# One copy for both value banks, early rows for two groups of expert blocks, and the last closing's transfers on another queue

## The chip, the cores and the metric

The kernel runs on one core of one Trainium2 chip. The core has a matrix engine (TensorE, PE in the profile), a vector engine (VectorE, DVE), an activation engine (ScalarE, ACT), a general engine (GpSimd, POOL) and an engine that mostly issues transfers (SyncE, SP). Each works through its own instructions in order, and they wait for one another by semaphores. The metric is the device time of one launch in microseconds (us); lower is better.

## What is computed

Two images of 256 channels and 3136 positions each go through two layers; all data are 32-bit floats. The first layer is a convolutional attention without softmax, which the kernel folds into one 256x256 matrix per image. The second is a transformer block over the 3136 positions as tokens:

```python
t = tokens(x)                                      # (2, 3136, 256)
# causal attention, 4 heads of 64
qkv = layernorm(t) @ W_attn
att = softmax(where(causal, q @ k.T / 8, lowest))
t = t + (att @ v) @ W_proj
# 8 experts, each token through its best two
probs = softmax(layernorm(t) @ gate_w + gate_b)
top2_vals, top2_idx = top_k(probs, 2)
for e in range(8):
    y = gelu(layernorm(t) @ W1[e] + b1[e]) @ W2[e] + b2[e]
    t = t + cw[:, e] * y                           # cw: top2_vals at top2_idx, else 0
```

The kernel doesn't run all tokens through all experts: it sorts the 12,544 pairs of token and expert into blocks of 128 rows by expert, and runs 102 such blocks in its main loop.

## The kernel before: the parts concerned

**Attention.** For each image `b`, each of 7 stretches `i` of W = 448 queries and each pair of heads `hp`, the kernel goes through blocks `j` of 128 keys. A step makes scores (PE), their exponentials `st` (ACT, from a ring of 5 buffers), adds these into `acc` (DVE), and three steps later multiplies them with the values into `yp` (PE). The matrix engine works on two halves of the keys at a time, so `yp` has two banks, one for each half, which have to be added at the end. `yp` exists once: the next stretch or pair of heads can't begin its values before `yp` has been read. There are 2 x 2 x 7 = 28 such endings, called closings here. (`...` marks cuts.)

```python
psc = pool(att, "psc", bufs=2, space=PSUM)     # scores: two buffers
py = pool(att, "py", bufs=1, space=PSUM)       # yp: one
fst = pool(att, "fst", bufs=5)                 # st
...
def values(n):
    ...
        yps[hp, i] = py.tile([P, 2, 512], F32, tag="y", name=f"yp_{sn}")
    ...
    if last:
        yh = qT[:, hp, i * W : (i + 1) * W]
        nc.scalar.copy(yh, yp[:, 0, :W])                            # L703
        nc.vector.tensor_tensor(yh, yh, yp[:, 1, :W], ALU.add)      # L704
        del yps[hp, i]
        later.append((clock[0], sum_rows, hp, i, yh))

def queue_of(hp, i):
    return nc.gpsimd if (b, hp, i) == (B - 1, NH - 1, NB - 1) else nc.sync
```

What follows a closing is a chain of small steps for the softmax's denominators, each put off by some steps through the list `later`: `sum_rows` sums `acc` over the keys (PE, L720), copies the sums out (ACT, L725) and sends them through HBM to bring them into another layout (L728, L731); `invert` takes the reciprocal (DVE, L740) and sends it back, spread over partitions (L741, L746); `scale` multiplies (DVE, L752); `hand_on` lets the output projection (`project_out`, L602) go on. For the very last of the 28 closings `queue_of` sends all these transfers by GpSimd's queue.

**The last closing, between the expert blocks.** When attention's own loop has ended, the chain of the last closing is run by `closing`, a generator from which `pull` takes pieces; between two expert blocks `meanwhile` pulls two or three pieces:

```python
def closing():
    if not general:
        while finished[B - 1][NH - 1] < N:
            clock[0] += 4
            due(clock[0])        # 1: sum_rows, 2: invert, 3: scale, 4: hand_on
            yield True
            yield True
        while not projected[B - 1]:
            yield False
        queue.append(judge())
    end.close()
    scatter_rows.append(...)
    yield True

def meanwhile():
    scatters = placed[1] and not sent[1]
    pull(3 if scatters or worked[0] >= MIXED else 2)
    ...
```

The pieces that follow are the output projection of image 1's last rows, then `dispatch(1)` (the gate's softmax, the two best experts and each pair's place, all on DVE; `placed[1]` is set at its end), then the scatter of image 1's rows into their places by GpSimd (`sent[1]` at its end). The rows of image 1 are first fetched for block 42, six blocks ahead of use.

**The expert blocks.** The loop over `n`, from -1 on:

```python
for n in range(-1, MAIN + LATE):                       # LATE = 3
    while len(fetched) * GB <= min(n + 6, MAIN - 1):   # GB = 3 blocks in a group
        fetched.append(fetch(len(fetched)))
    ...
    if 0 <= n < MAIN:
        act[n] = hidden(n, xin.pop(n), wb.pop(n))      # PE L1403, ACT gelu L1412
    for m in (n + 1, n + 2):
        ... xin[m] = inputs(m, groups[m // GB])        # PE transposes L1380, ACT copy L1384
    for m in (n + 1, n + 2):
        ... wb[m] = weights(m)                         # DVE copy of the expert's W1, L1391, two buffers
    if 0 <= n - LATE < MAIN:
        outputs(n - LATE, act.pop(n - LATE))           # PE L1422, DVE bias L1432
    ...
    between()                                          # meanwhile

def fetch(g):
    ...
    if g == 0:
        return early_rows, None      # rows of blocks 0 to 2, loaded during attention (tokens, L1659)
    ...
        (nc.sync if g > 2 else nc.scalar).dma_start(   # L1329
            out=xb, in_=xds[b][s * P : e * P].rearrange("(n p) w -> p n w", p=P))
```

The buffers `xb` of the groups from 1 on lie in memory that attention gives back at its end, so their transfers start only then.

Of the kernel before, what the change touches and what calls it, by code (L numbers as in the profile page):

```python
# [27 lines left out]
def conv_attn_moe_kernel(  # L28
# [75 lines left out]
    MIXED = MOST0 + E  # L104
    NBLK = (2 * B * N + E * (P - 1)) // P
    GB = 3

    MAIN = NBLK - GB
    SCALE = 1.0 / HS**0.5
# [333 lines left out]
    def layer1(nm, general):  # L443

        with ExitStack() as whole:
# [170 lines left out]
            def attend(  # L616
# [63 lines left out]
                def values(n):  # L680
                    i, hp, j, first, last, order = steps[n]
                    k = chunk(j)
                    c0 = max(0, j * P - i * W)
                    sn = f"{nm}{b}_{hp}_{i}"
                    st = sts.pop(n)
                    if first:
                        yps[hp, i] = py.tile([P, 2, 512], F32, tag="y", name=f"yp_{sn}")
                    yp = yps[hp, i]

                    for h in range(0, k, HS):  # L690
                        end = last or (h and all(chunk(o) <= h for o in order[order.index(j) + 1 :]))
                        for a in range(2):
                            nc.tensor.matmul(  # L693
                                yp[a * HS : (a + 1) * HS, h // HS, c0:W],
                                v[hp][h : h + HS, j, a, :HS],
                                st[h : h + HS, a, c0:],
                                start=first,
                                stop=bool(end),
                            )
                    if last:  # L700

                        yh = qT[:, hp, i * W : (i + 1) * W]
                        nc.scalar.copy(yh, yp[:, 0, :W])  # L703
                        nc.vector.tensor_tensor(yh, yh, yp[:, 1, :W], ALU.add)  # L704
                        del yps[hp, i]
                        later.append((clock[0], sum_rows, hp, i, yh))

                def queue_of(hp, i):

                    return nc.gpsimd if (b, hp, i) == (B - 1, NH - 1, NB - 1) else nc.sync  # L710

                def sum_rows(hp, i, yh):
                    r = (b * NH + hp) * NB + i
                    sn = f"{nm}{b}_{hp}_{i}"
                    acc = accs.pop((hp, i))
                    sp = bank(f"sp_{b}_{hp}_{i}")

                    flat = acc.rearrange("p a w -> p (a w)")
                    for g in range(4):
                        nc.tensor.matmul(  # L720
                            sp[g * 32 : (g + 1) * 32, : W // 2], ones[:, :32],
                            flat[:, g * W // 2 : (g + 1) * W // 2], start=True, stop=True,
                        )
                    line = fs.tile([P, W], F32, tag="rb", bufs=3, name=f"line_{sn}")
                    nc.scalar.copy(line[:, : W // 2], sp[:, : W // 2])  # L725
                    halves = sum_d[r].rearrange("a (h w) -> (a h) w", h=2)
                    for g in range(4):
                        queue_of(hp, i).dma_start(  # L728
                            out=halves[g : g + 1], in_=line[g * 32 : g * 32 + 1, : W // 2]
                        )  # L730
                    queue_of(hp, i).dma_start(  # L731
                        out=sums[:, r], in_=sum_d[r].rearrange("a (p f) -> (a p) f", p=HS)
                    )
                    later.append((clock[0] + 4, invert, hp, i, yh))

                def invert(hp, i, yh):
                    r = (b * NH + hp) * NB + i
                    sn = f"{nm}{b}_{hp}_{i}"
                    back = fs.tile([P, 2 * W // P], F32, tag="back", name=f"back_{sn}")
                    nc.vector.reciprocal(back, sums[:, r])  # L740
                    queue_of(hp, i).dma_start(  # L741
                        out=inv_d[r].rearrange("a (p f) -> (a p) f", p=HS), in_=back
                    )
                    rb = fs.tile([P, W], F32, tag="rb", bufs=3, name=f"rb_{sn}")
                    for a in range(2):
                        queue_of(hp, i).dma_start(  # L746
                            out=rb[a * HS : (a + 1) * HS], in_=inv_d[r, a].partition_broadcast(HS)
                        )
                    later.append((clock[0] + 4, lambda hp, i, yh: scale(hp, i, yh, rb), hp, i, yh))
# [551 lines left out]
            def experts(w1s, w2s, b2s, ex, es, ps6, between, need, written):  # L1301
# [4 lines left out]
                def fetch(g):  # L1306
                    s, e = g * GB, (g + 1) * GB
                    b = 0 if e <= FULL0 else 1
                    need(b)
                    if g == 0:  # L1310
                        return early_rows, None
                    f = known[b][0]
                    xb = ex.tile([P, GB, xds[b].shape[1]], F32, tag="xb", bufs=3, name=f"xb_{nm}_{g}")
                    if b:
                        at = nc.values_load_multi_w_load_instructions(
                            qblk[0:1, s - f : e - f],
                            engines=(SP,),
                            min_val=0,
                            max_val=NBLK - FULL0 - 1,
                            skip_runtime_bounds_check_because="a permutation's places",  # L1320
                        )[1]
                        table = xds[b].rearrange("(n p) w -> n p w", p=P)
                        for a in range(GB):
                            nc.sync.dma_start(
                                out=xb[:, a],
                                in_=table[bass.ds(at[a], 1)].rearrange("o p w -> p (o w)"),
                            )
                    else:
                        (nc.sync if g > 2 else nc.scalar).dma_start(  # L1329
                            out=xb, in_=xds[b][s * P : e * P].rearrange("(n p) w -> p n w", p=P)  # L1330
                        )
                    mixed = max(0, min(e, MIXED) - s) if b else 0
                    other = None
                    if mixed:
                        other = ex.tile([P, GB, C], F32, tag="xo", bufs=1, name=f"xo_{nm}_{g}")
                        nc.sync.dma_start(
                            out=other[:, :mixed],
                            in_=xds[0][s * P : (s + mixed) * P].rearrange("(n p) w -> p n w", p=P),
                        )
                    return xb, other  # L1340
# [33 lines left out]
                def inputs(n, group):  # L1374
                    xb, to = group
                    g = n % GB
                    rows = xb[g] if n < GB else xb[:, g, :C]
                    tp = ps6.tile([P, 512], F32, tag="tp", bufs=2, name=f"tp_{nm}_{n}")
                    for c in range(NH):
                        nc.tensor.transpose(  # L1380
                            tp[:, c * P : (c + 1) * P], rows[:, c * P : (c + 1) * P], ident
                        )
                    xT = es.tile([P, NH, P], F32, tag="xT", name=f"xT_{nm}_{n}")
                    nc.scalar.copy(xT.rearrange("p c t -> p (c t)"), tp[:, : NH * P])  # L1384
                    return xT, to
# [252 lines left out]
            def tokens(b, qT, done):  # L1638
# [5 lines left out]
                if b == 0:  # L1644
# [8 lines left out]

                    while not read[B - 1]:
                        yield False
                    for n in range(0, GB, 2):
                        m = min(2, GB - n)
                        xb = bg.tile([P, 2, C], F32, tag="xn", name=f"xb_{nm}_first{n}")
                        nc.sync.dma_start(  # L1659
                            out=xb[:, :m],  # L1660
                            in_=xds[0][n * P : (n + m) * P].rearrange("(n p) w -> p n w", p=P),
# [108 lines left out]
            def closing():  # L1770

                if not general:
                    while finished[B - 1][NH - 1] < N:
                        clock[0] += 4
                        due(clock[0])
                        yield True
                        yield True
                    while not projected[B - 1]:
                        yield False
                    queue.append(judge())  # L1780
# [5 lines left out]
            with ExitStack() as moe:  # L1786
# [11 lines left out]
                        )  # L1798
                for _ in load_w2(True):
                    pass  # L1800
                while len(early_rows) < GB:
                    pull()

                def need(b):
# [9 lines left out]
                    queue.appendleft(finish(1, oy, 3))  # L1814

                def meanwhile():
                    scatters = placed[1] and not sent[1]
                    pull(3 if scatters or worked[0] >= MIXED else 2)
                    if side and next(side[0], None) is None:
                        side.popleft()  # L1820

# [179 lines left out]
```

## Time and profile before

| | before |
|---|---|
| time, median of 3 runs | 1307.98 us |
| lowest, highest | 1307.3, 1308.54 us |
| span of the profiled execution | 1331.2 us |
| PE busy | 1276.9 us (96%) |
| DVE busy | 787.7 us (59%) |
| ACT busy | 602.2 us (45%) |
| POOL busy | 306.2 us (23%) |
| mean granted PE clock | 0.989 |

The profile is one execution, recorded by the hardware; the recorded execution is some 23 us longer than the timed ones. Times in it are microseconds from its start, unless a row says mean ns. Attention runs from about 97 to 887 us, the expert blocks from 888 to 1311 us. A row names the engine, the line of the kernel, the operation and the tiles (`out<-in`); in brackets stands for how long the engine had been idle before, and what ended that.

### The profile page before, as it was taken

To read this page: it belongs to the slowest core of one execution; us is meant where nothing else is said; L and a number is where in the kernel's file an instruction comes from. 1 tells how busy PE (TensorE), PEld (TensorE's weight loads), DVE (VectorE), ACT (ScalarE), POOL (GpSimd) and SP (SyncE) were. 2 spreads that over 40 slices of the span, in tenths; PEclk is the share of its full clock that TensorE was granted. 3 is DMA by queue.
4 is the path that set the end of the run, shared out by engine and by line. 5 is a ranking of instruction groups with operands and counts; after the bars stand their busy time and mean duration, and the time that the engine had idled before them with its cause. 6 is when DMAs were issued, how large, how long until landed. Compare 5 with 4: busy or idle time off the path is not lost.

```text
span 1331.2 us, 28014 instructions
## 1 busy us (share of the span) xinstructions
PE 1276.9 (96%) x10569; PEld 808.0 (61%) x10569; DVE 787.7 (59%) x1683; ACT 602.2 (45%) x1226; POOL 306.2 (23%) x297
## 2 busy tenths in 40 slices
PE   8999999999999999999999989989999999899995
PEld 7875444444444444444345434449988999899894
DVE  1582555748777654675768777765744443355553
ACT  0145554555565554455553455553423333244341
POOL 1113110000000111110004461010066212655541
PEclk9999999999999999999999999999999999999997
DMA  9993000000000000100001126141244433556553
GB/s 311 383 326 113 16 24 24 24 16 24 9 17 17 17 2 9 40 9 15 9 8 60 60 80 198 33 138 56 67 144 129 130 109 97 179 175 202 180 156 107
DMA packets 110471, 123.54 MB, mean 93 GB/s; under 512 B 19904, under 2 KB 100045, under 8 KB 110329
## 3 DMA queue, kind: packets, MB, share of 16 engines
q1 hardware_dynamic: 96232, 92.49, 22.4%
q0 software_dynamic: 10272, 26.00, 5.8%
q10 hardware_dynamic: 3824, 3.18, 0.8%
q8 instruction: 87, 1.43, 0.5%
q14 instruction: 56, 0.45, 0.1%
HBM read 62.65 MB, written 60.41 MB: 92 GB/s over the span
## 4 chain that ended last, share of the span: by engine, by line
PE 91%; DVE 3%; issue 2%; ACT 1%; DMA 1%; POOL 0%; DVEq 0%; SPq 0%; POOLq 0%; ACTq 0%
PE yp_f L693 20%; PE sc_f L653 19%; PE ht_f L1403 14%; PE yp_f L1422 13%; PE qk_f L539 7%; PE v_f L558 4%; PE pp_f L602 4%; PE cp L324 3%; PE gram L255 3%; PE tp_f L1380 2%; DVE acc_f L675 1%; ACT st_f L661 1%; PE sp_f L720 1%; PE yo_f L1549 1%; PE xp_f L518 1%
## 5 line engine op out<-in xcount | busy, mean ns | idle before, releaser
L661 ACT ACTIVATE st_f<-sc_f 128x896 f32<-128x896 f32 (+5 forms) x400 | 333.5, 838 | 300.1 <-PE sc_f L653 273.7
L675 DVE TENSOR_TENSOR acc_f<-acc_f,st_f 128x896 f32<-128x896 f32 (+5 forms) x372 | 366.5, 985 | 168.3 <-ACT st_f L661 161.3
L693 PE MATMUL yp_f<-st_f,v_f 64*64 64x448 f32 (+6 forms) x3184 | 340.5, 503 | 9.7 <-DVE qT_f L704 6.5
L653 PE MATMUL sc_f<-qT_f,kT_f 64*64 64x448 f32 (+6 forms) x3184 | 341.5, 500 | 4.0 <-ACT st_f L661 4.0
L1412 ACT ACTIVATE g_f<-ht_f,b1b 128x128 f32<-128x128 f32 x408 | 116.8, 371 | 243.0 <-PE ht_f L1403 127.6
L1403 PE MATMUL ht_f<-xT_f,w_f 128*128 128x128 f32 x1632 | 203.4, 277 | 9.3 <-issue 6.6
L653 PEld LDWEIGHTS sc_f<-qT_f,kT_f 64*64 64x64 f32 x3184 | 116.6, 133 | 156.4 <-issue 134.5
L693 PEld LDWEIGHTS yp_f<-st_f,v_f 64*64 64x64 f32 x3184 | 112.3, 133 | 162.6 <-issue 134.7
L1403 PEld LDWEIGHTS ht_f<-xT_f,w_f 128*128 128x128 f32 x1632 | 198.5, 193 | 14.9 <-issue 10.4
L501 POOL TENSOR_SCALAR xn_f<-t 128x256 f32<-128x256 f32 (+1 forms) x50 | 68.2, 1373 | 542.6 <-issue 330.8
L1284 POOL DMA_INDIRECT x_slots<-xr_f,idx x100 | 113.0, 1130 | 218.7 <-DVE xr_f L1276 116.6
L1391 DVE COPY w_f<-w1s_f 128x1024 f32 x102 | 71.1, 698 | 86.8 <-PE ht_f L1403 38.8
L539 PE MATMUL qk_f<-px_f,wat 128*128 128x512 f32 (+1 forms) x224 | 92.6, 558 | 1.2 <-ACT px_f L524 1.2
L1439 POOL DMA_INDIRECT y_tokens<-ys_f,to_f x60 | 60.3, 1005 | 139.7 <-DVE ys_f L1432 109.8
L1432 DVE TENSOR_TENSOR ys_f<-yp_f,kT_f 128x128 f32<-128x128 f32 x102 | 29.6, 291 | 99.7 <-PE yp_f L1422 65.3
L663 DVE TENSOR_TENSOR st_f<-st_f,keep 128x256 f32<-128x256 f32 (+1 forms) x112 | 44.2, 395 | 68.2 <-ACT st_f L661 67.7
L539 PEld LDWEIGHTS qk_f<-px_f,wat 128*128 128x128 f32 x224 | 38.7, 190 | 54.4 <-issue 45.3
L1422 PE MATMUL yp_f<-px_f,g_f 128*128 x204 | 62.7, 390 | 1.0 <-issue 1.0
L1422 PE MATMUL yp_f<-v_f,g_f 128*128 x204 | 61.5, 382 | 0.8 <-issue 0.8
L1422 PE MATMUL yp_f<-kT_f,g_f 128*128 x204 | 62.1, 386 | 0.0
L1422 PE MATMUL yp_f<-w2s_f,g_f 128*128 x204 | 61.2, 382 | 0.3 <-issue 0.3
L1496 POOL DMA_INDIRECT y_f<-y_slots,idx x50 | 54.8, 1096 | 16.3 <-issue 14.7
(259 smaller groups left out, 1170.8 us busy)
## 6 DMA issues: line engine op xcount, KB each, us to landing
x_slots<-fill SPq DMA_DIRECT2D x1, 8127.0 KB
xb_f<-x_slots SPq DMA_DIRECT2D x60, 129.0 KB
x_slots<-fill SPq DMA_DIRECT2D x1, 7296.0 KB
y_slots<-ys_f SPq DMA_DIRECT2D x57, 128.0 KB
kept<-t SPq DMA_DIRECT2D x2, 3200.0 KB
x<-in_x_dram SPq DMA_DIRECT2D x14, 448.0 KB
xr<-in_x_rows_dram SPq DMA_DIRECT2D x12, 512.0 KB
out_dram<-ot_f SPq DMA_DIRECT2D x24, 256.0 KB
```

The lines of the kernel that those rows point to most:

```text
L501: nc.gpsimd.tensor_scalar(xn[:k, a], ts[b][:k, n + a, :C], ts[b][:k, n + a, MEAN : MEAN + 1], ts[b][:k, n + a, RSTD : RSTD + 1], ALU.subtr ...
L539: nc.tensor.matmul(ps[:, :w], wat[:, c, d0 : d0 + P], xT[:, c, :w], start=(c == 0), stop=(c == NH - 1),)
L653: nc.tensor.matmul(ps[h : h + HS, a, c0:W], kT[hp][rows, j * P + h : j * P + h + HS], qT[rows, hp, q0 + c0 : q0 + W], start=True, stop=True,)
L661: nc.scalar.activation(st[:k, :, c0:], ps[:k, :, c0:W], AF.Exp, scale=SCALE)
L675: nc.vector.tensor_tensor(acc[:k, :, c0:], acc[:k, :, c0:], st[:k, :, c0:], ALU.add)
L693: nc.tensor.matmul(yp[a * HS : (a + 1) * HS, h // HS, c0:W], v[hp][h : h + HS, j, a, :HS], st[h : h + HS, a, c0:], start=first, stop=bool( ...
L1284: s = nc.gpsimd.indirect_dma_start(out=xds[b], out_offset=bass.IndirectOffsetOnAxis(ap=idxs[b][:kk, k, n : n + 1], axis=0), in_=xr[:kk], i ...
L1391: nc.vector.tensor_copy(w, w1s[:, :, bass.ds(e, 1), :].rearrange("p c e h -> p c (e h)"))
L1403: nc.tensor.matmul(ht[:, k, :], w[:, c, k * P : (k + 1) * P], xT[:, c, :], start=(c == 0), stop=(c == NH - 1),)
L1412: nc.scalar.activation(g[:, k, :], ht[:, k, :], AF.Gelu, bias=b1bs[b][:, k, i : i + 1])
L1422: nc.tensor.matmul(yp[:, :C], g[:, k, :], w2s[k][:, bass.ds(e, 1), :].rearrange("p e d -> p (e d)"), start=(k == 0), stop=(k == KH - 1),)
L1439: s = nc.gpsimd.indirect_dma_start(out=y_tokens, out_offset=bass.IndirectOffsetOnAxis(ap=to[:, n % GB : n % GB + 1], axis=0), in_=ys, in_o ...
```

## The change

Three things are changed.

1. **Both banks in one copy.** ACT copies both banks of `yp` at once (128x896) into a buffer `both` from the ring of the `st` tiles, and GpSimd adds the two halves from there into `yh`. DVE has no part in a closing's first step any more. Before, `yp` was free when DVE's addition had ended; now it is free when ACT's copy has.
2. **Early rows for two groups.** The rows of the first six expert blocks, and not three, are loaded during attention. The three more blocks take buffers of the `xn` and `xr` tiles that are idle by then. Group 1 is no longer fetched when attention ends.
3. **The last closing.** Its transfers go by SP's queue like those of all others. `closing` gives six pieces (three blocks) between the sums and the reciprocal, four (two blocks) between the reciprocal and the scaling, and none after that, where it gave two each. To make up for the later start, the sorting of image 1's tokens (`dispatch(1)`) takes three pieces per block from its start on and not only from its scatter on.

```diff
--- before.py
+++ after.py
@@ -104,6 +104,7 @@
     MIXED = MOST0 + E
     NBLK = (2 * B * N + E * (P - 1)) // P
     GB = 3
+    EARLY = 2
 
     MAIN = NBLK - GB
     SCALE = 1.0 / HS**0.5
@@ -700,14 +701,11 @@
                     if last:
 
                         yh = qT[:, hp, i * W : (i + 1) * W]
-                        nc.scalar.copy(yh, yp[:, 0, :W])
-                        nc.vector.tensor_tensor(yh, yh, yp[:, 1, :W], ALU.add)
+                        both = fst.tile([P, 2, W], F32, tag="st", name=f"both_{sn}")
+                        nc.scalar.copy(both, yp[:, :, :W])
+                        nc.gpsimd.tensor_tensor(yh, both[:, 0], both[:, 1], ALU.add)
                         del yps[hp, i]
                         later.append((clock[0], sum_rows, hp, i, yh))
-
-                def queue_of(hp, i):
-
-                    return nc.gpsimd if (b, hp, i) == (B - 1, NH - 1, NB - 1) else nc.sync
 
                 def sum_rows(hp, i, yh):
                     r = (b * NH + hp) * NB + i
@@ -725,10 +723,10 @@
                     nc.scalar.copy(line[:, : W // 2], sp[:, : W // 2])
                     halves = sum_d[r].rearrange("a (h w) -> (a h) w", h=2)
                     for g in range(4):
-                        queue_of(hp, i).dma_start(
+                        nc.sync.dma_start(
                             out=halves[g : g + 1], in_=line[g * 32 : g * 32 + 1, : W // 2]
                         )
-                    queue_of(hp, i).dma_start(
+                    nc.sync.dma_start(
                         out=sums[:, r], in_=sum_d[r].rearrange("a (p f) -> (a p) f", p=HS)
                     )
                     later.append((clock[0] + 4, invert, hp, i, yh))
@@ -738,12 +736,12 @@
                     sn = f"{nm}{b}_{hp}_{i}"
                     back = fs.tile([P, 2 * W // P], F32, tag="back", name=f"back_{sn}")
                     nc.vector.reciprocal(back, sums[:, r])
-                    queue_of(hp, i).dma_start(
+                    nc.sync.dma_start(
                         out=inv_d[r].rearrange("a (p f) -> (a p) f", p=HS), in_=back
                     )
                     rb = fs.tile([P, W], F32, tag="rb", bufs=3, name=f"rb_{sn}")
                     for a in range(2):
-                        queue_of(hp, i).dma_start(
+                        nc.sync.dma_start(
                             out=rb[a * HS : (a + 1) * HS], in_=inv_d[r, a].partition_broadcast(HS)
                         )
                     later.append((clock[0] + 4, lambda hp, i, yh: scale(hp, i, yh, rb), hp, i, yh))
@@ -1307,8 +1305,8 @@
                     s, e = g * GB, (g + 1) * GB
                     b = 0 if e <= FULL0 else 1
                     need(b)
-                    if g == 0:
-                        return early_rows, None
+                    if g < EARLY:
+                        return early_rows[s:e], None
                     f = known[b][0]
                     xb = ex.tile([P, GB, xds[b].shape[1]], F32, tag="xb", bufs=3, name=f"xb_{nm}_{g}")
                     if b:
@@ -1374,7 +1372,7 @@
                 def inputs(n, group):
                     xb, to = group
                     g = n % GB
-                    rows = xb[g] if n < GB else xb[:, g, :C]
+                    rows = xb[g] if n < EARLY * GB else xb[:, g, :C]
                     tp = ps6.tile([P, 512], F32, tag="tp", bufs=2, name=f"tp_{nm}_{n}")
                     for c in range(NH):
                         nc.tensor.transpose(
@@ -1653,9 +1651,12 @@
 
                     while not read[B - 1]:
                         yield False
-                    for n in range(0, GB, 2):
-                        m = min(2, GB - n)
-                        xb = bg.tile([P, 2, C], F32, tag="xn", name=f"xb_{nm}_first{n}")
+                    for n, m in ((0, 2), (2, 2), (4, 1), (5, 1)):
+                        name = f"xb_{nm}_first{n}"
+                        if m == 2:
+                            xb = bg.tile([P, 2, C], F32, tag="xn", name=name)
+                        else:
+                            xb = bg.tile([P, C], F32, tag="xr", name=name).unsqueeze(1)
                         nc.sync.dma_start(
                             out=xb[:, :m],
                             in_=xds[0][n * P : (n + m) * P].rearrange("(n p) w -> p n w", p=P),
@@ -1770,11 +1771,13 @@
             def closing():
 
                 if not general:
+
+                    blocks = deque((3, 2))
                     while finished[B - 1][NH - 1] < N:
                         clock[0] += 4
                         due(clock[0])
-                        yield True
-                        yield True
+                        for _ in range(2 * blocks.popleft() if blocks else 0):
+                            yield True
                     while not projected[B - 1]:
                         yield False
                     queue.append(judge())
@@ -1798,7 +1801,7 @@
                         )
                 for _ in load_w2(True):
                     pass
-                while len(early_rows) < GB:
+                while len(early_rows) < EARLY * GB:
                     pull()
 
                 def need(b):
@@ -1814,8 +1817,8 @@
                     queue.appendleft(finish(1, oy, 3))
 
                 def meanwhile():
-                    scatters = placed[1] and not sent[1]
-                    pull(3 if scatters or worked[0] >= MIXED else 2)
+                    sorting = projected[1] and not sent[1]
+                    pull(3 if sorting or worked[0] >= MIXED else 2)
                     if side and next(side[0], None) is None:
                         side.popleft()
```

## The prediction

> **What bounds the kernel now.** I read the page's shares first, then the waits of PE, then the timeline at the closings, then the chain and the stretches around the end of attention.
>
> ```profile
> PE 1276.9 (96%) x10569; PEld 808.0 (61%) x10569; DVE 787.7 (59%) x1683; ACT 602.2 (45%) x1226; POOL 306.2 (23%) x297
> ```
>
> PE is busy for 1276.9 of 1331.2 us, so 54.3 us is all the idle time there is. The change takes no matrix work away; it can only win back part of these 54.3 us. By the waits of PE, the two parts can reach these rows:
>
> ```profile
> PE yp_f L693 <- DVE qT_f L704: 6.5, 6, 1.5
> PE sc_f L653 <- ACT st_f L661: 4.0, 3, 1.5
> PE ht_f L1403 <- DVE w_f L1391: 2.7, 1, 2.7
> PE tp_f L1380 <- DMA xb_f<-x_slots: 1.1, 1, 1.1
> ```
>
> The columns are total us, times and longest. The first row is the closing's wait for DVE's addition: only 6 of 28 closings leave PE idle. The third and fourth happen once each, just after attention. A closing that does wait, the first (timeline, start and length ahead of the engine; the weight loads of PE left out):
>
> ```profile
> 130.16 0.53 ACT L703 COPY qT_f<-yp_f 128x448 f32<-128x448 f32 x1
> ...
> 130.75 0.82 DVE L675 TENSOR_TENSOR acc_f<-acc_f,st_f 128x640 f32<-128x640 f32 x1
> ...
> 131.50 0.61 DVE L704 TENSOR_TENSOR qT_f<-qT_f,yp_f 128x448 f32<-128x448 f32 x1
> 132.03 0.42 DVE L663 TENSOR_TENSOR st_f<-st_f,keep 128x256 f32<-128x256 f32 x1
> 132.16 0.61 PE L693 MATMUL yp_f<-st_f,v_f 64*64 64x448 f32 x4 [1.49 <-DVE qT_f L704]
> ```
>
> ACT's copy ends at 130.69, but DVE, in order, is in the middle of an `acc` addition, so `yp` is free only at 132.11. In most closings the same release comes 1.76 us after the copy's start, and PE covers it with two score products and the sums (at 316.16 the addition ends at 317.91, and PE goes on at 317.98 without a gap).
>
> The end of attention, from the chain of waits in that stretch:
>
> ```profile
> 889.00 2.10 POOL sums L728 x3
> 891.10 3.76 DMA sums<-line_f
> ...
> 895.52 1.97 DMA sums<-sums
> 897.49 0.02 issue
> 897.51 0.07 DVE back_f L740
> ...
> 897.70 0.71 DVE w_f L1391
> 898.40 0.14 issue
> 898.54 2.99 PE ht_f L1403 x16
> ```
>
> The reciprocal was put into DVE's order right after the sums were sent. It waits until 897.51, and the weight copy of block 3 behind it makes PE wait 2.69 us. A block's hidden layer takes 1.78 us later in the chain; here it takes 2.99, because the granted clock has dropped (stretches: length, then busy time of PE, PEld, DVE, ACT, POOL, then PEclk, DMA share, GB/s):
>
> ```profile
> 894.00:899.00 5.00, 2.31 (x21) 2.10 (x20) 0.88 (x2) 1.71 (x6) 1.14 (x2) 1.00 0.02 1
> 899.00:904.00 5.00, 5.00 (x25) 4.66 (x25) 0.43 (x1) 1.41 (x5) 1.07 (x2) 0.66 0.15 47
> ```
>
> **What the Trainium skill says.** "TensorE: Matmul & The Clock Gate", Part 1: after an idle window the array's clock falls to half and comes back after some 3.4 us of work. The trace agrees: 0.66 in the 5 us after the gap. So a gap costs more than its own length. "DMA: Bandwidth & Descriptors", Latency and other measured facts: the first byte takes about 0.6 us from SP's queue and 1 us from GpSimd's. The trace agrees in direction: an issue of the sums lasts 0.25 us on SP and 0.56 on POOL (medians of L728). "GPSIMD Engine Reference", sections 1 and 3.1: GpSimd can't read PSUM, hence the copy first, and an addition of two 2048-wide tiles takes it 4.5 us against DVE's 2.3. No two-input operation runs on POOL in this trace; its one-input normalisation of 128x256 takes 1.37 us, or 5.3 ns per element. "SBUF — State Buffer", Who interferes with whom: GpSimd and a DVE operation with two inputs block each other. Here DVE's 128x896 additions that overlap a normalisation take 1.08 to 1.24 us, against 1.09 otherwise: little to see.
>
> **Part 1, one copy for both banks.** Removed: 28 DVE additions of 0.615 us, 17 us of an engine with slack. Longer: 28 ACT copies. I take the 128x896 exponential's 0.92 us (mean 918 ns) for the 128x896 copy, against 0.53 before: 28 x 0.39 = 11 us more on ACT, beside PE. Added: 28 POOL additions. By the skill's rate the estimate is 4.5 x 448/2048 = 1.0 us, by this trace's normalisation 448 x 5.3 ns = 2.4 us.
>
> On the path: `yp` is free 0.92 us after the copy's start. For the six closings that wait I take the gain in release (old end of addition, less copy start plus 0.92), at most the recorded wait:
> - at 130.16: 132.11 - 131.08 = 1.03, of a wait of 1.49
> - at 197.25: 1.36, wait 1.02, so 1.02
> - at 515.55: 1.04, of 1.49
> - at 585.83: 1.38, wait 1.02, so 1.02
> - at 634.61: 1.61, wait 0.59, so 0.59
> - at 695.62: 1.88, wait 0.85, so 0.85
>
> The sum is 5.55 us. Weight loads wait for L704 in 14 places, so other closings may lose a tenth each that the modelled ends hide: 0.5 more. Against it: in a closing ACT's exponentials come 0.39 later. In the full-size closing at 316.16 they would end at 318.0 and 319.3, needed at 319.5 and 321.0, so nothing is lost; in the small closings (first stretches, 6 of them) I allow 0.1 each, 0.6. Part 1: -5.5 us.
>
> **Part 2, group 1 early.** It removes the 1.15 us wait of PE for `xb` at 893.4. The first group's early loads are issued at 826.7, 60 us ahead of use; the second group's will stand beside them.
>
> **Part 3, the last closing.** Without gaps, from 888.23 a block's hidden layer and transposes take 2.0 us, and outputs 1.73. Hidden layers 0 to 3 would then run to about 896.3, the outputs of block 0 to 898.1. In the trace these end at 903.99, so 5.9 us can be won: 1.15 (part 2) + 2.69 (weights) + some 2.0 of slow clock (1.2 on the hidden layer, 0.7 on what follows). Does the new order avoid the wait? SP can issue the sums at 888.8. With four issues of 0.25 us and about 2 us to land (the 1.97 above), they arrive about 892; the second transfer about 894.4. The reciprocal now stands behind the weight copy of block 4, which can't start before hidden layer 2 has ended (894.1), so it runs at about 895 with little wait. `inverses` lands at about 897.6 and `rb` near 900.5; the scaling stands behind the bias of block 1 at about 902.3. But nothing is left between scaling and projection: the second of the two projected tiles needs the scaled rows, and I charge 0.4 us. Net for parts 2 and 3: -5.5 us.
>
> The faster sorting: the pieces of `dispatch(1)` took DVE about 20 us in all, two per block; three per block are 2.8 us a block on average, plus weights and bias 1.2, that is 4.0 against PE's 3.73. The worst triple is about 3.7 + 1.2 = 4.9. A weight copy has 5.6 us between its buffer coming free and its use, so I expect this backlog to stay hidden. The dispatch begins one block later and takes about 3.5 fewer, so the scatter should end some 2.5 blocks (9 us) earlier than 1043.5. It was in time before; the gain from that is none.
>
> **Sum.** -5.5 - 5.5 = -11.0 us of profiled time. The timed runs are 23 us shorter than the profile, so some of its waits may be its own; I keep 85%, -9.4, giving 1298.5 us.
>
> **Rivals.** (a) *`both` holds up the ring.* `both` is an extra claim on five `st` buffers and comes back only after POOL's addition. For it: POOL works in order, and its scatters run back to back around the closing at 775. Against it: the buffer is needed again four steps, some 6 us, later. If it bites in half of the closings by 0.5 us, 7 us of the gain are lost: 1305. (b) *ACT becomes the release.* The score buffers are two, and PE already waits 4.0 us for exponentials; 0.39 us more, 28 times, unhidden would be 11 us: about 1309. Against it: ACT idles 0.59 us in each steady step. (c) *SP is no faster.* SP's queue is loaded with weights at 885 to 887, and the transfers keep landing late; then the reciprocal still waits and only parts 1 and 2 count: about 1303. (d) *DVE's heap of sorting pieces starves PE*: 2 to 4 us lost, 1301.
>
> **Range and chances.** Rivals cost singly up to 10 us; the upside is the full idle time of both places, 14 us. So 1294 to 1305. All idle time of PE is only 4% and the reachable part under 1%, so a change over 2% either way is very unlikely: faster 0.02, same 0.97, slower 0.01.
>
> **What would show it.** Right: no PE wait for L704, few for the new copy; the copy near 0.92 us; no PE gap over 0.5 us from 887 to 905 and a clock of 1.00 there; the outputs of block 0 over 5 us sooner after the end of attention; the scatter's end some 9 us earlier. Wrong: ACT waits for POOL's addition at the `st` ring, more PE waits for `st_f` L661, DVE still blocked at L740 or L752, or new gaps between 925 and 960. A gain under 3 us, or a loss, would make the reasoning wrong, and not only its size.

## The result

| | before | after |
|---|---|---|
| time, median of 4 runs each, side by side | 1308.26 us | 1303.21 us |
| lowest to highest | 1307.3 to 1309.54 | 1302.95 to 1303.32 |
| ratio, with its 95% interval | | 0.996 (0.9943 to 0.9978) |
| span of the profiled execution | 1331.2 us | 1301.6 us |

The gain is 5.05 us, 0.4%. The time lies inside the predicted range, but the gain is about half of the 9.4 us predicted.

The profile after answers to the rows shown of before. The page's shares:

```profile
PE 1267.3 (97%) x10569; PEld 802.9 (62%) x10569; DVE 792.2 (61%) x1655; ACT 610.6 (47%) x1226; POOL 344.9 (26%) x317
```

The waits of PE (total us, times, longest):

```profile
PE yo_f L1547 <- DVE y_f L1534: 8.2, 5, 4.9
...
PE xp_f L519 <- POOL xn_f L502: 2.2, 2, 1.2
...
PE sc_f L654 <- ACT st_f L662: 0.9, 2, 0.7
PE yp_f L694 <- ACT both_f L705: 0.9, 2, 0.4
...
PE ht_f L1401 <- ACT xT_f L1382: 0.6, 1, 0.6
```

The waits for DVE's addition, for the weights at the end of attention and for `xb` are gone; what took over is 0.9 us for the new copy and 0.6 for a copy of transposed rows. But the second row shown is new: PE waits for POOL's normalised tiles, and no recording of the kernel before has such a row. No rival had this one.

The first closing (timeline: start, length, in brackets the idle time ahead):

```profile
129.03 0.90 ACT L705 COPY both_f<-yp_f 128x896 f32<-128x896 f32 x1
...
129.98 1.52 PE L694 MATMUL yp_f<-st_f,v_f 64*64 64x448 f32 x16 [0.44 <-ACT both_f L705]
130.01 1.43 POOL L706 TENSOR_TENSOR qT_f<-both_f 128x448 f32<-128x448 f32 x1 [4.93 <-ACT both_f L705]
```

PE goes on 0.95 us after the copy's start, and 2.00 before (132.16 - 130.16). POOL's addition begins as PE's next values do and holds nobody here. Over all 28 it takes 1.30 us on average (36.3 us in all), between the two estimates.

The end of attention (stretches: length, then busy time of PE, PEld, DVE, ACT, POOL, then PEclk, DMA share, GB/s):

```profile
885.00:890.00 5.00, 4.94 (x40) 4.87 (x41) 1.50 (x3) 3.57 (x15) 0.00 (x0) 1.00 0.05 5
890.00:895.00 5.00, 5.00 (x33) 4.63 (x33) 1.45 (x4) 1.96 (x8) 0.00 (x0) 1.00 0.52 138
895.00:900.00 5.00, 5.00 (x34) 4.46 (x33) 3.41 (x10) 1.41 (x5) 0.00 (x0) 1.00 0.12 39
```

No gap is left, at full clock. So both places look as predicted, and yet only half of the time came. The experiments ask where the rest is.

### The profile page after: what moved, and what is told of

Read it like the earlier page. It is cut to its first block, busy times and chain, and to the rows that moved or that the text cites. A ratio compares the mean times of both kernels' runs of the same rounds, so it can differ in the third digit from the quotient of the medians.

```text
span 1301.6 us, 28033 instructions
## 1 busy us (share of the span) xinstructions
PE 1267.3 (97%) x10569; PEld 802.9 (62%) x10569; DVE 792.2 (61%) x1655; ACT 610.6 (47%) x1226; POOL 344.9 (26%) x317
## 4 chain that ended last, share of the span: by engine, by line
PE 89%; DVE 3%; issue 3%; ACT 2%; POOL 2%; DMA 1%; DVEq 0%; POOLq 0%; ACTq 0%; SPq 0%
PE yp_f L694 20%; PE sc_f L654 19%; PE ht_f L1401 13%; PE yp_f L1420 12%; PE qk_f L540 7%; PE v_f L559 4%; PE pp_f L603 4%; PE cp L325 3%; PE gram L256 3%; PE tp_f L1378 2%; PE sp_f L718 1%; ACT st_f L662 1%; PE yo_f L1547 1%; PE xp_f L519 1%; DMA y_f<-y_slots,idx 1%
## 5 line engine op out<-in xcount | busy, mean ns | idle before, releaser
L676 DVE TENSOR_TENSOR acc_f<-acc_f,st_f 128x896 f32<-128x896 f32 (+5 forms) x372 | 375.3, 1009 | 160.0 <-ACT st_f L662 151.0
L1401 PE MATMUL ht_f<-xT_f,w_f 128*128 128x128 f32 x1632 | 199.5, 275 | 0.6 <-ACT xT_f L1382 0.6
L706 POOL TENSOR_TENSOR qT_f<-both_f 128x448 f32<-128x448 f32 x28 | 36.3, 1298 | 522.7 <-ACT both_f L705 522.7
L502 POOL TENSOR_SCALAR xn_f<-t 128x256 f32<-128x256 f32 (+1 forms) x50 | 72.3, 1455 | 143.6 <-DVE t L171 47.2
```

Source lines behind the costliest of these rows:

```text
L502: nc.gpsimd.tensor_scalar(xn[:k, a], ts[b][:k, n + a, :C], ts[b][:k, n + a, MEAN : MEAN + 1], ts[b][:k, n + a, RSTD : RSTD + 1], ALU.subtr ...
L676: nc.vector.tensor_tensor(acc[:k, :, c0:], acc[:k, :, c0:], st[:k, :, c0:], ALU.add)
L1401: nc.tensor.matmul(ht[:, k, :], w[:, c, k * P : (k + 1) * P], xT[:, c, :], start=(c == 0), stop=(c == NH - 1),)
```

## The experiments

The fifth to eighth kernels of the table ran on another chip, on which the kernel before takes 2.3% longer (1337.87 us), so times are compared within a set only.

| kernel | time, us | before in the same set | ratio, 95% interval |
|---|---|---|---|
| before once more | 1307.63 | 1307.97 | 0.9996 (0.9987 to 1.0004) |
| part 1 alone | 1306.15 | 1307.97 | 0.9986 (0.9979 to 0.9992) |
| part 2 alone | 1307.11 | 1307.97 | 0.9995 (0.9987 to 1.0003) |
| part 3 alone | 1305.73 | 1307.97 | 0.9981 (0.9972 to 0.9989) |
| part 3, SP's queue alone | 1337.77 | 1337.87 | 0.9996 (0.9985 to 1.0008) |
| part 3, spacing and sorting alone | 1336.02 | 1337.87 | 0.9985 (0.9973 to 0.9998) |
| after, addition on DVE | 1331.66 | 1337.87 | 0.9959 (0.9945 to 0.9972) |
| after, normalisation first | 1327.09 | 1337.87 | 0.9925 (0.9898 to 0.9952) |
| after once more | 1302.98 | 1307.08 | 0.997 (0.9957 to 0.9982) |
| after, normalisation first, again | 1299.13 | 1307.08 | 0.9939 (0.9926 to 0.9953) |
| the same with eight transfers more | 1296.66 | 1307.08 | 0.9916 (0.9902 to 0.9929) |
| the same with GpSimd's queue in the last closing | 1296.74 | 1307.08 | 0.9923 (0.991 to 0.9937) |

### The kernel before once more

No edit. The recorded execution of before was 23 us longer than the timed ones. This asks which of its waits are the kernel's own (theory A in the texts on record: the waits were read rightly, and the change brings new ones) and which belong to that execution (theory B).

> The kernel before, unchanged, recorded once more. Theory A (the waits were read rightly, and the change itself brings new ones): the recorded span is again near 1331 us, with about 6.5 us of PE waiting for the closing's addition L704, 2.7 for the weights behind the reciprocal and some 9 us of PE idle marked issue in the expert blocks. Theory B (that recorded execution was a disturbed one, 23 us over the timed runs): the span is near 1307 us, the issue rows are gone, and the waits that the change removes are smaller than the 6.5 + 2.7 + 1.1 us read.

Measured: a span of 1306.1 us. The waits of PE in it:

```profile
PE yp_f L693 <- DVE qT_f L704: 8.5, 7, 1.6
...
PE ht_f L1403 <- DVE w_f L1391: 2.5, 1, 2.5
PE tp_f L1380 <- DMA xb_f<-x_slots: 1.4, 1, 1.4
...
PE pp_f L602 <- DVE qT_f L752: 0.7, 1, 0.7
```

and the stretch of the gap at the end of attention:

```profile
890.00:895.00 5.00, 2.51 (x23) 2.30 (x22) 0.88 (x2) 1.40 (x5) 1.14 (x2) 1.00 0.03 1
```

The waits that the change removes are all there, and larger (8.5 us at seven closings, for 6.5 at six). What is not there: the expert blocks' rows of PE waiting for "issue", that is, for nothing that the profile shows (9.7 us in the recorded execution of before: 6.6 for `ht`, 2.1 for the experts' `yp`, 1.0 for `tp`; the row of 6.6 is below), the 4.0 us of waits for exponentials, and a slow clock after the gap; the clock stays at 1.00 through 890 to 905. So the removable waits were the kernel's own, and much of the 23 us was not.

```profile
PE ht_f L1403 <- issue: 6.6, 10, 1.0
```

The slow clock is another matter. It came back after the same gap when part 1 alone was recorded (below), and with part 2 alone too (0.68 in the same stretch); what decided it is in the last section.

```profile
890.00:895.00 5.00, 5.00 (x25) 4.84 (x26) 0.00 (x0) 1.41 (x5) 1.08 (x2) 0.68 0.15 47
```

### Each part alone

Part 1 alone: the copy of both banks and POOL's addition (the diff's lines at L700), all else as before.

> Part 1 alone: both banks in one ACT copy, addition on GpSimd. Theory A: -5.5 us from the closings, +3 to 4 us lost where GpSimd's normalisation now stands behind the addition (PE waits for xn, 2.2 us in the changed kernel's record), so -1.5 to -2.5 us against before. Theory B: below -1.5 us, or a small loss, because the closings' waits were smaller in the timed runs.

Part 2 alone: `EARLY`, the four early loads and the two uses of `early_rows`.

> Part 2 alone: rows of six blocks loaded during attention. Theory A: -1 us at most (PE's one wait for xb, 1.1 us), less if the wait for the weights just behind it grows by as much (then 0). Theory B: 0 us.

Part 3 alone: SP's queue, the spacing of three and two blocks, and the sorting by three pieces.

> Part 3 alone: last closing's transfers on SP, wider spacing, sorting at three pieces. Theory A: -4.5 us (2.7 of waiting for the weights and 2 of slow clock, less 0.3 between scaling and projection). Theory B: -2 to -3 us, because the timed runs lose less there. The wait of PE for xb, 1.1 us, stays in both.

Measured: 1.8, 0.9 and 2.2 us under before. The sum is 4.9 us, about as much as the whole change brings, so the parts add up as far as these intervals tell.

*Part 2* brings nothing that its interval would show. PE's wait for `xb` (1.4 us) is gone, but the next one grows, since the reciprocal that ends it comes no earlier: the wait for the weights is 3.1 us here for 2.5. By the trace 0.8 us is left.

*Part 1* I followed by the starts of the closings' copies, less those of the kernel before once more (negative is earlier). Between the first closing (+0.3) and the thirteenth (-1.8, at 447 us) and again from the fourteenth (+0.6, at 497) to the last (-3.0) time is won: 2.1 and 3.6, that is 5.7. But between the thirteenth and the fourteenth 2.3 us are lost. There image 1 begins, and there is the new wait for POOL. POOL's timeline in the kernel before:

```profile
286.97 2.88 POOL L501 TENSOR_SCALAR xn_f<-t 128x256 f32<-128x256 f32 x2 [44.94 <-PE xp_f L518]
454.17 5.16 POOL L501 TENSOR_SCALAR xn_f<-t 128x256 f32<-128x256 f32 x4 [164.32 <-issue]
```

With nothing else to do, POOL had normalised the second two of image 1's tiles at 287 (and the first two at 239), over 160 us before their use. In the changed kernel:

```profile
445.87 1.25 POOL L706 TENSOR_TENSOR qT_f<-both_f 128x448 f32<-128x448 f32 x1 [39.14 <-ACT both_f L705]
447.11 10.07 POOL L502 TENSOR_SCALAR xn_f<-t 128x256 f32<-128x256 f32 x7
```

In POOL's order the normalisation stands behind the additions of the closings of image 0, down to the thirteenth. POOL idles for 39 us and then has to do it in a hurry, while PE waits twice. (By the closings part 1 wins 3.4 us, and timed 1.8; the recorded execution, 1304.95 us, is 1.2 us faster than the median of its runs.)

*Part 3* I followed by the starts of the bias of each block's output (DVE). The lead over the kernel before is 4.5 us at block 4, about 4.0 at block 13 and from 30 to 58, and then falls to about 2 in blocks 59 to 65, where the first rows of the output are gathered. This second loss is in the changed kernel too (1.3 us there).

### The pieces of part 3

SP's queue alone:

```diff
-    return nc.gpsimd if (b, hp, i) == (B - 1, NH - 1, NB - 1) else nc.sync
+    return nc.sync
```

> The kernel before, with only the last closing's transfers moved from GpSimd's queue to SP's. Theory order (the wait for weights is lost because the reciprocal stands too early in DVE's order): the sums come about 2 us earlier on SP, but the reciprocal still blocks the weight copy of block 3, so PE's wait for weights shrinks from 2.5 us to somewhere from 0.5 to 1.5 and does not go; 1306.5 to 1307.6 us, 0.5 to 1.5 under the kernel before. Theory queue (SP alone does it): the wait is under 0.3 us and the time is that of the last part alone, about 1305.7. And for the 1.8 us that the last part loses again in blocks 59 to 65: if the change of queues brings it, the first gather of finished rows starts over 5 us after block 56's bias here; if not, 3.1 us after, as before.

The spacing and the sorting alone, the transfers still on GpSimd's queue:

```diff
+    blocks = deque((3, 2))
...
-        yield True
-        yield True
+        for _ in range(2 * blocks.popleft() if blocks else 0):
+            yield True
...
-    scatters = placed[1] and not sent[1]
-    pull(3 if scatters or worked[0] >= MIXED else 2)
+    sorting = projected[1] and not sent[1]
+    pull(3 if sorting or worked[0] >= MIXED else 2)
```

> The kernel before, with the last closing's reciprocal and scaling put three and two blocks behind and the sorting pulled three pieces at a time, but its transfers still on GpSimd's queue. Theory order: the wait for weights (2.5 us) goes as in the last part alone; about 1305.7 us, 2.0 to 2.5 under the kernel before, unless the later landing makes DVE stand before the reciprocal: then up to 1 us less is won. Theory queue: the sums land at 897.5 as before, DVE waits there, and PE waits 1 us or more for a later weight copy: 1306.5 or more. And for the 1.8 us lost again in blocks 59 to 65: if the earlier sorting brings it, the first gather of finished rows starts over 5 us after block 56's bias here; if the queues do, 3.1 us after.

Measured: nothing (0.9996) for the queue, 1.85 us for the spacing. The waits of PE at the end of attention, first with the queue alone, then with the spacing alone:

```profile
PE ht_f L1403 <- DVE w_f L1391: 1.8, 1, 1.8
```

```profile
PE tp_f L1380 <- DMA xb_f<-x_slots: 1.9, 1, 1.9
```

With SP's transfers 1.8 us of the wait for weights stay (a little more than I had expected); with the spacing that wait is gone, and the only larger one is that which part 2 removes. So it is the place of the reciprocal in DVE's order that counts. The intervals of the two timings overlap, and it is the traces that tell them apart; the spacing and the sorting were not run singly. And the second loss: the first gather starts 5.75 us after block 56's bias with the queue alone, 3.14 with the spacing alone. It comes with the queue, not with the sorting.

### The addition on DVE, and the normalisation first

After, with the two banks added by DVE from `both`:

```diff
-    nc.gpsimd.tensor_tensor(yh, both[:, 0], both[:, 1], ALU.add)
+    nc.vector.tensor_tensor(yh, both[:, 0], both[:, 1], ALU.add)
```

> The changed kernel, with the closing's addition of the two copied banks on DVE (28 more additions of some 0.6 us there, none on POOL). Theory POOL order (the normalisation of image 1 waits in POOL's order behind the last closings of image 0): the loss between the closings at 446 and 497 goes, PE's wait for the normalised tiles is under 0.3 us, and the time is 2.0 to 3.9 us under the changed kernel's 1303.2: 1299.3 to 1301.2. Theory ACT (the longer copy, 0.91 for 0.53 us, holds the exponentials and makes that loss): the loss stays and the time is 1303 or, by the additions on DVE, more.

After, with the first two normalisations of image 1 put into POOL's order ahead of the additions of the closings at 405 and 446 (`-1` only marks the point; the rest of `project_qkv` is as it was):

```diff
-    normalise()
+    normalise(); yield -1            # project_qkv
...
     def before_block(i):
         need(b, min(i, NS - 1))
+        if i == NB - 1 and b + 1 < B:
+            next(pieces[b + 1])
```

> The changed kernel with the addition kept on POOL, and the first two normalisations of image 1 put ahead of the last two closings of image 0 in POOL's order. Theory POOL order: as with the addition on DVE, the loss between 446 and 497 goes, and the time is 2.0 to 3.9 us under the changed kernel's 1303.2. Theory sharing (GpSimd's addition slows DVE's additions beside it[...], whatever the order): the time stays at 1303.2 within 0.7, while the version with the addition on DVE gains.

Measured: the wait for POOL is gone in both. Against the kernel before once more, their closings lose nothing between the twelfth and the fourteenth, across the start of image 1 (leads of 3.2 and 3.3 us with DVE, 2.5 and 2.6 with the normalisation first), where the changed kernel falls from 3.0 us ahead to 1.2 behind. The sharing theory said that only DVE's version would gain; the version that keeps the addition on POOL gains at least as much (0.75% for 0.41%), so sharing isn't the cause. The size for DVE's version stays open: 0.41% is what the changed kernel has anyway. Its recorded execution shows a pause of 5.0 us of ACT at 778 whose end the profile puts to "remote", and a wait for weights of 1.9 us, and the changed kernel didn't run on that chip. So the normalisation first was run again beside the changed kernel.

### The normalisation first, beside the changed kernel

> The changed kernel once more, as the base of the three others. Both theories: 0.995 to 0.997 of the kernel before; the first gather of finished rows 5.7 us after block 56's bias.

> The changed kernel with the first two normalisations of image 1 ahead of the last two closings of image 0, once more, now beside the changed kernel. Theory POOL order: 2.0 to 3.9 us under the changed kernel. Theory sharing: within 0.7 us of it.

Measured: 3.85 us less than the changed kernel, 1299.13 for 1302.98. In the trace, POOL's and PE's rows at the start of image 1 in the version with the normalisation first:

```profile
446.95 3.42 POOL L502 TENSOR_SCALAR xn_f<-t 128x256 f32<-128x256 f32 x2
...
450.14 0.86 PEld L519 LDWEIGHTS xp_f<-ident,xn_f 128*128 128x128 f32 x8 [0.70 <-issue]
450.15 1.09 PE L519 MATMUL xp_f<-ident,xn_f 128*128 128x128 f32 x8
```

All eight transposes run through. By the closings, 2.67 us are won there against the second recording of the changed kernel. The timed difference is larger, and the two recorded executions of the changed kernel show a likely reason. The first:

```profile
452.18 0.44 PE L519 MATMUL xp_f<-ident,xn_f 128*128 128x128 f32 x2 [1.16 <-POOL xn_f L502]
453.62 0.69 PE L519 MATMUL xp_f<-ident,xn_f 128*128 128x128 f32 x2 [1.00 <-POOL xn_f L502]
454.25 1.77 PE L694 MATMUL yp_f<-st_f,v_f 64*64 64x448 f32 x8
...
457.10 0.92 PE L694 MATMUL yp_f<-st_f,v_f 64*64 64x448 f32 x8
```

The second:

```profile
453.28 0.44 PE L519 MATMUL xp_f<-ident,xn_f 128*128 128x128 f32 x2 [1.00 <-POOL xn_f L502]
453.65 0.98 PE L694 MATMUL yp_f<-st_f,v_f 64*64 64x448 f32 x8
```

The waits are the same (1.16 and 1.00). In the first execution the products after them take 1.77 us for 0.98, and 0.92 again from 457 on; this costs 1.55 us more by the closings. The first took 1303.3 us, the second 1300.6, only 1.6 more than the recorded execution with the normalisation first (1299.0). The other five runs of the changed kernel beside the second took 1302.3 to 1303.9 at a mean clock of 0.992 or 0.993, for its 0.994, so the slow clock may be the usual case, but no trace shows it: two of the four runs beside the first took 1303.2 and 1303.3 at 0.994. "TensorE: Matmul & The Clock Gate", Part 1, of the Trainium skill says that the window by which the clock is set runs freely, so that the same program can differ from run to run; the two traces agree, and so does its time of some 3.4 us for coming back (here 453.6 to about 457). It asks for an idle window of some 3.4 us too, and there the trace differs: waits of 1.16 and 1.00 us were enough once.

### What went through GpSimd's queue

The late gather appeared in every kernel with SP's transfers in the last closing, and in no other, whatever else it had. Eight transfers fewer go from GpSimd's queue there. So, on top of the normalisation first, eight small ones were given back, early, to rows that nothing reads:

```diff
+    if (b, hp, i) == (0, NH - 1, 2):
+        for k in range(8):
+            nc.gpsimd.dma_start(out=pad_d[k : k + 1], in_=line[:1, : W // 2])
```

> The same, and eight small transfers of 224 elements more on GpSimd's queue, early (in a closing of image 0 near 200 us), to rows that nothing reads. The first gather has been late in every kernel that sends eight transfers fewer from GpSimd's queue, and in no other. Theory count (the number of earlier transfers on that queue sets when the gather runs): the first gather is 3.1 us after block 56's bias again, and the time is 1 to 1.8 us under the one without the pads. Theory closing (it is the early end of the last closing, or SP's longer list): the gather stays at 5.7 us and the time is the same or up to 0.5 us more.

And, also on top of the normalisation first, `queue_of` as in the kernel before:

> As the one with the normalisations first, but with the last closing's transfers on GpSimd's queue as before, its reciprocal and scaling still three and two blocks behind. Theory count: the first gather is at 3.1 us; the wait for weights does not come back, or up to 1 us of it; the time is 0.3 to 1.8 us under the one with SP's transfers. Theory queue needed (SP's faster landing is what removes the wait for weights): PE waits 1.5 us or more for weights in blocks 3 to 6, and the time is the same or more than with SP's transfers.

Measured: 1296.66 and 1296.74 us, 2.5 and 2.4 under the version without. This is more than the 1 to 1.8 us expected, and more than the loss by the traces (1.3 us in the changed kernel, 1.9 with the normalisation first); the rest isn't placed. The first gather is 3.04 and 3.03 us after block 56's bias, for 5.67. POOL's timeline with the normalisation first, without the eight transfers:

```profile
1105.19 0.97 POOL L1437 DMA_INDIRECT y_tokens<-ys_f,to_f  x1 [2.76 <-DVE eq_f L1350]
1110.10 1.47 POOL L1494 DMA_INDIRECT y_f<-y_slots,idx  x1 [3.94 <-PE ht_f L1401]
```

and with them:

```profile
1103.60 1.00 POOL L1441 DMA_INDIRECT y_tokens<-ys_f,to_f  x1 [4.32 <-issue]
...
1108.04 1.05 POOL L1498 DMA_INDIRECT y_f<-y_slots,idx  x1 [1.31 <-DMA y_slots<-ys_f]
```

POOL stands still for about 4 us once in this stretch in both. Without the eight, this falls on the first gather, which ought to start 1.3 us after the scatter ahead of it. With them it falls on a scatter two transfers earlier (block 55's), whose usual wait is 2.76 us and which nobody waits for. In the kernel before it falls on a scatter as well (4.30 us, block 53). So the count or the size of what went through the queue before moves it; what the pause is, no run here shows.

GpSimd's queue in the last closing costs only 0.5 us there (PE waits for the scaled rows), once the reciprocal is well placed. SP's queue brought no more than it cost. Both versions beat both kernels; the best takes 0.9916 of the kernel before.

## Why the prediction was half right

In the sum, the mechanism was right: both places where PE could win were named with what holds it there, and the working for each survives in an undisturbed execution. The changed kernel's two side effects taken away, the gain is 10.4 us (1296.66 for 1307.08), close to the 11.0 us of the sum before its 85%. That it is so close is in part luck: the closings gave more than charged (6.3 us for 5.5), and the slow clock nothing where 2.0 were charged. What failed are the terms that aren't in the sum.

- **Part 1, -5.5.** The waits won are larger: seven closings with 8.5 us; less 0.9 for the copy and 0.9 for exponentials, which stand in the place of the 0.6 charged, 6.7 are left. Measured between the first and the last closing, with the normalisation first: 7.14 - 0.80 = 6.3. The step "Against it", which looked for costs only in ACT's exponentials, missed the cost of POOL's order: 2.7 us of waits, and 1.5 more of slow clock in one of two recordings. I had written under rival (a) that POOL works in order, and followed that fact only to the `st` ring. The right question was what POOL had been doing ahead of time.
- **Part 2, the 1.15.** Won (1.4 in the undisturbed execution) together with part 3; alone 0.8 of it is left, since the wait for the weights grows.
- **Part 3, -5.5 with part 2.** Measured 4.2 from the last closing's copy to block 58's bias (241.41 less 237.25). The weights' 2.69 held (2.5). The 2.0 of slow clock is the mis-sized term: it was charged as if it came every time, and it measured nothing in the undisturbed execution, which ran at 1.00 after a gap of 2.5 us. Parts 1 and 2 alone did have it, after gaps of 2.8 and 3.1 us; how often the timed runs have it, no run shows. Against that, the 0.4 charged between scaling and projection did not come, and a wait of 0.7 there goes that the first recorded execution hadn't shown. So 2.5 + 1.4 + 0.7 = 4.6 are won by block 4 (4.6 measured), and 0.5 is given back up to block 13, in the stretch that the sorting by three pieces fills, which I had expected to stay hidden; that the sorting takes it is argued from the place.
- **When things land in part 3.** Counted from the first issue of the sums (predicted at 888.8, measured at 880.68, so 8.1 later in the prediction): reciprocal predicted 895, measured 887.75 + 8.1 = 895.9; scaling 902.3, measured 903.3. The scatter's end comes 8.7 us earlier against the blocks, 9 was predicted, with no gain, as said.
- **A transfer moved to another queue** had no cost in my working. It moved POOL's pause onto the first gather: 1.3 us.
- **The 85%** doubted the waits that were read, because of the 23 us by which the recorded execution was longer. The waits held (8.5, 2.5 and 1.4 us); of what was summed only the slow clock did not. That the time still lies inside the range is luck: the range was drawn for the rivals, and none of the three costs that came (2.7, 1.5 and 1.3 us) was among them.

By the traces: -6.3 - 4.2 + 2.7 + 1.5 + 1.3 = -5.0 us; measured -5.05. The recorded executions (1306.1 and 1301.6) lie 4.5 us apart, so that the two agree to 0.05 says little. Rival (c) was nearest in time, 1303, but its reason was not met: DVE never stood long before the reciprocal. Rivals (a) and (b) show as 0.9 us of waits for exponentials at most, (d) as the 0.5 at most.

## What to carry to other kernels

An engine that works in order and is mostly idle may be running far ahead in silence; before it is given a new task that waits for others, look for what it now does early, and put that ahead of the new task. When a chain of transfers makes others wait, first move its consumer in the waiting engine's order: that, with the faster sorting, brought 1.85 us here (part 3 as a whole 2.2, on another chip), and the faster queue alone none. A recorded execution longer than the timed ones should be recorded again before its waits are summed up.

## What was not expected of the hardware

- Around the first gather, GpSimd pauses once for about 4 us between indirect transfers (4.30, 3.94, 4.32 us in three kernels), and what has gone through its queue before decides where. It falls on the 112th indirect transfer of the launch in the kernel before, on the 116th with eight transfers fewer in that queue, and on the 114th with eight of one row added.
- Two waits of 1.16 and 1.00 us in 3 us halved the granted clock in one execution (0.98 to 1.77 us for the same products) and not in another. What the traces say about it stands below the list.
- The same kernel takes 1307.97 us on one chip and 1337.87 on another, where PE's records have short gaps put to "issue" (4.9 us in eight places for the experts' `yp` in the kernel with SP's queue alone). The recorded execution of before looks like that chip's; that it was one is only argued.
- GpSimd's addition of two 128x448 tiles takes 1.30 us. The estimate from "GPSIMD Engine Reference", section 3.1, was 1.0.

**Where a gap falls.** Within a trace, the clock's changes during the work lie whole multiples of 3.41 us apart (in the first recording of the changed kernel 443.73 us, 130 of them, at full clock, then one of them at half). Cut along these points, the stretch with the two waits is, in the first and in the second recording (length, busy time of PE, PEld, DVE, ACT, POOL, then PEclk, DMA share, GB/s):

```profile
450.08:453.49 3.41, 1.38 (x10) 0.60 (x6) 2.05 (x2) 1.40 (x2) 3.41 (x3) 1.00 0.03 5
```

```profile
449.19:452.60 3.41, 1.93 (x18) 0.67 (x10) 2.18 (x2) 1.77 (x3) 3.41 (x3) 1.00 0.04 6
```

In the first, PE was busy for 1.38 us of the stretch, and the next one ran at half clock. In the second, the same waits fell across two stretches (1.93 and 2.73 us busy), and the clock stayed at 1.00. It is the same after attention: 0.64 and 0.96 us busy with parts 1 and 2 alone, and half clock next; 2.25 and 2.08 us in the kernel before once more, where the gap of 2.5 us fell across two stretches, and full clock. So in these recordings the same gap cost more or not by where it fell. An exact limit isn't shown: on the other chip a stretch with about 1.6 us busy (893.06 us, SP's queue alone) was followed by full clock, and one with 1.85 (965.87 us, the normalisation first) by half.
